# Two groups of 512 edges a step, and ScalarE copying the transposed sums out of two PSUM banks, in a graph layer on one core

## The chip, the cores and the metric

The kernel runs on one core of a Trainium2 chip. The metric is the device time of an execution in microseconds; the median of three runs before the change is 1433.29 us (1432.50 to 1433.74). The engines go by the profile's names: PE is TensorE (PEld its weight loads), DVE is VectorE, ACT is ScalarE, POOL is GpSimd, SP issues transfers.

## What is computed

One message-passing layer of a graph network with a residual and a layer norm: 6250 nodes of 128 features, 100000 edges sorted by destination. Cut to what matters:

```python
msg_in = concatenate([x[src], x[dst]])            # 100000 x 256
h = relu(msg_in @ Wm1 + bm1)                      # 256 wide
h = relu(h @ Wm2 + bm2)
messages = h @ Wm3 + bm3
agg = segment_sum(messages, dst) / clip(count, 1)
upd = relu(concatenate([x, agg]) @ Wn1 + bn1) @ Wn2 + bn2
out = layernorm(x + (x + upd))
```

## The kernel before

The kernel has three stages. The first makes two tables in memory from x: `atab`, x times the upper half of Wm1 (one row of 256 fp32 a node), and `btab`, x times the lower half, split into three bf16 terms. The second, the edge loop, goes over 196 groups of 512 edges (the last has 256 places). The third handles the nodes in blocks of up to 512.

In the edge loop a group is four subgroups of 128 edges. As the edges are sorted, the destinations of a subgroup lie in a window of 21 nodes (WB) that begins at a number read from `tilei`. For one group:

- `fetch` issues four gathers on POOL (L387), each 128 rows of `atab` by source into `ag`, and four transfers on SP (L393) of the windows' `btab` rows into `bw`. Both tiles have four buffers (pool `ld`), one a group.
- `destinations` issues, for two groups at a time, two transfers on ACT's queue (L328) that spread the destinations over partitions into `db`.
- `hot` makes on DVE two one-hot matrices by comparison: `oht` (L408), which picks `bw` rows for the edges, and `oh` (L411), which sums edges by destination.
- `first_layer` transposes the `ag` rows on PE into `ph` (L424, two halves of 64 rows side by side) and adds `bw` times `oht` there (L430). ACT adds the bias and clips (L435) into `h1`. `ph` has two banks, one for each half of a group (pool `p1`).
- `second_layer` multiplies `h1` by `w2` on PE (L444) into `ph2`, two banks, and DVE clips into `h2` (L446), of which there are four (NH2). A column of ones stands behind the 256 in `h2`, so that edges are counted with the sums.
- `sums` multiplies `oh` by `h2` on PE (L453) into the bank `pg` (pool `pa`, one), four strips of 32 rows, one a subgroup; ACT copies it to `part` (L456).
- `add_up` transposes `part` on PE (L464) into two banks `pt`, and DVE adds each window of 21 columns from `pt` to `acc` in SBUF (L469, four a group), at a place given by a register.

Each matmul in fp32 of L424, L444, L453 and L464 in the source stands as two instructions in the trace where it is a product (L444 has eight in the source and 16 in the trace), and as one where it is a transpose.

The order on PE is written out by hand (`tc.manual_schedule`): what the loop at L500 calls is what PE runs, in this order. The loop is a pipeline over groups with `ahead, lag = 2, 3`. Step i fetches group i, and with g = i - 2 then runs `hot` of g, `add_up` of g - 4, `first_layer` of g, `sums` of g - 3, `second_layer` of g - 1. So each step has one group in each function, every one from another group, and a product of ACT or DVE has about a step or more until PE reads it. On ACT, DVE, POOL and SP the tile framework places instructions by its own priorities; for ACT and DVE the order is that of the program until step 6 (`turns`). A buffer's next writer waits for its last reader, on whichever engine. [...]

Of the kernel before, what the change touches and what calls it, by code (L numbers as in the profile page):

```python
# [9 lines left out]
F32 = mybir.dt.float32  # L10
# [5 lines left out]
ENG = mybir.EngineType  # L16
PSUM = bass.MemoryType.PSUM
# [10 lines left out]
def kernel(  # L28
# [16 lines left out]
):  # L45

# [323 lines left out]
    with edge, tc.tile_pool(name="wk", bufs=2) as wk, tc.tile_pool(  # L370
        name="p1", bufs=2, space=PSUM
    ) as p1, tc.tile_pool(name="p2", bufs=2, space=PSUM) as p2, tc.tile_pool(
        name="pa", bufs=1, space=PSUM
    ) as pa, tc.tile_pool(name="pt", bufs=2, space=PSUM) as ptp:


        NH2 = 4
# [40 lines left out]
        def first_layer(ag, bw, oht, nt):  # L418
# [14 lines left out]
            for c in range(HC):  # L433
                for h in range(nh):
                    nc.scalar.activation(h1[:, c, h * 2 * P:(h + 1) * 2 * P], phs[h][:, c, :], AF.Relu,  # L435
                                         bias=b1[:, c:c + 1])
# [11 lines left out]
        def sums(oh, h2, nt):  # L448

            n = nt * WN  # L450
            pg = pa.tile([P, H + 1], F32, name="pg")
            for j in range(nt):
                nc.tensor.matmul(pg[j * WN:(j + 1) * WN, :], oh[:, j, :], h2[:, j, :],  # L453
                                 start=True, stop=True, skip_group_check=True)
            part = wk.tile([P, H + 1], F32, name="part")
            nc.scalar.copy(part[:n, :], pg[:n, :])  # L456
            return part

        def add_up(part, firsts, nt):
            pts = [ptp.tile([P, HC + 1, NQ], F32, name="pt") for _ in range(nt // 2)]  # L460
            for c in range(HC + 1):
                for h, pt in enumerate(pts):
                    rows = part[halves[h], c * P:(c + 1) * P] if c < HC else part[halves[h], H:].to_broadcast([NQ, P])
                    nc.tensor.matmul(pt[:, c, :], rows, ident[halves[h], halves[h]], is_transpose=True,  # L464
                                     start=True, stop=True, skip_group_check=True)
            for j, first in enumerate(firsts):
                window = acc[:, :, ds(first, WB)]
                k = j % 2 * WN
                nc.vector.tensor_add(window, window, pts[j // 2][:, :, k:k + WB])  # L469
# [28 lines left out]
        ahead, lag = 2, 3  # L498
        st = {}
        for i in range(NG + ahead + lag + 1):  # L500
            if i == 6:
                turns.close()
            if i == 16:
                late_loads()
                none = wk.tile([16, (NG * GE - E) // 16], I32, name="none", bufs=1)
                nc.vector.memset(none, NONE)
                nc.sync.dma_start(dpad[:E].rearrange("(p e) -> p e", p=16), dst.rearrange("(p e) -> p e", p=16))
                nc.sync.dma_start(dpad[E:].rearrange("(p e) -> p e", p=16), none)
            for step, after in enumerate((20, 24, 27)):
                if i >= after and (i - after) % 8 == 0 and (i - after) // 8 < len(pieces):  # L510
                    double((i - after) // 8, step)
            if i < NG:
                nt = GT if i < NGF else LT
                firsts = load_bases(tilei[0:1, i * GT:(i + 1) * GT], nt, ENG.SP)
                if i == NGF:
                    dbs = last_destinations()
                elif i % 2 == 0:
                    dbs = early.pop(0) if early else destinations(i, min(2, NGF - i), dst_row)
                st[i] = dict(nt=nt, got=fetch(srcT[:, i, :], nt, firsts), db=dbs.pop(0))
            g = i - ahead  # L520
            if 0 <= g < NG:
                s = st[g]
                ag, bw = s.pop("got")
                oht, s["oh"] = hot(s.pop("db"), pbase[:, g, :], dloc[:, g, :s["nt"]], s["nt"])
            k = g - lag - 1
            if 0 <= k < NG:
                s = st.pop(k)
                if "firsts" not in s:
                    s["firsts"] = load_bases(tilei[0:1, k * GT:(k + 1) * GT], s["nt"], ENG.DVE)
                add_up(s["part"], s["firsts"], s["nt"])  # L530
            if 0 <= g < NG:
                s = st[g]
                s["h1"] = first_layer(ag, bw, oht, s["nt"])
            k = g - lag
            if 0 <= k < NG:
                s = st[k]
                s["part"] = sums(s["oh"], s["h2"], s["nt"])
            m = g - 1
            if 0 <= m < NG:
                s = st[m]  # L540
                s["h2"] = h2s[m % NH2]
                second_layer(s["h1"], s["h2"], s["nt"])
            if m == NG - 1:
                for k in range(NG - lag, NG):
                    s = st[k]
                    s["firsts"] = load_bases(tilei[0:1, k * GT:(k + 1) * GT], s["nt"], ENG.DVE)
        assert not st
# [9 lines left out]
        with tc.For_i(0, groups, 1) as g:  # L557
# [3 lines left out]
            with tc.For_i(0, more, 1):  # L561
# [17 lines left out]
                add_up(sums(oh, h2s[0], GT), load_bases(ti, GT, ENG.DVE), GT)  # L579
# [132 lines left out]
```

## Time and profile before

| | us |
|---|---|
| median of the runs | 1433.29 |
| the profiled execution's own time | 1215.18 |
| its span, first to last instruction | 1213.4 |
| first L424 starts | 93.42 |
| last L444 block starts | 1128.24 |
| node stage's first matmul (L618) starts | 1136.67 |
| mean granted TensorE clock of the profiled execution | 0.991 |

The profiled execution is 218 us shorter than the median of the runs. Durations are read from the former. The page's group rows give, for a line and an engine, the instructions' count, their busy time and mean duration. The timeline gives the start, the duration from the first start to the last end, and how many instructions of one kind were merged; in brackets, idle time of the engine just before and what ended it. Matmuls overlap: the start of the next one says more than the duration[...]. "64\*128" ahead of a matmul's output is rows by columns of the array that it uses.

### The profile page before, as it was taken

To read this page: it belongs to the slowest core of one execution; us is meant where nothing else is said; L and a number is where in the kernel's file an instruction comes from. 1 tells how busy PE (TensorE), PEld (TensorE's weight loads), DVE (VectorE), ACT (ScalarE), POOL (GpSimd) and SP (SyncE) were. 2 spreads that over 40 slices of the span, in tenths; PEclk is the share of its full clock that TensorE was granted. 3 is DMA by queue.
4 is the path that set the end of the run, shared out by engine and by line. 5 is a ranking of instruction groups with operands and counts; after the bars stand their busy time and mean duration, and the time that the engine had idled before them with its cause. 6 is when DMAs were issued, how large, how long until landed. Compare 5 with 4: busy or idle time off the path is not lost. (4 is left out here: it accounts for less than half of the span.)

```text
span 1213.4 us, 32800 instructions
## 1 busy us (share of the span) xinstructions
PE 1181.3 (97%) x11196; PEld 898.6 (74%) x11197; DVE 675.1 (56%) x2085; ACT 446.8 (37%) x1158; POOL 804.7 (66%) x859
## 2 busy tenths in 40 slices
PE   7998999999999999999999999999999999999896
PEld 5746777777777777777777777777777777777565
DVE  5763555555555555555555555555555555555686
ACT  4553333333333333333333333333333333333256
POOL 8266776777777777777777777777777777673220
PEclk9998999999999999999999999999999999999898
DMA  9875666666555555555555555555555555552333
GB/s 270 295 255 148 188 186 186 180 187 179 154 153 153 151 152 153 144 152 151 153 153 151 151 152 149 145 155 153 153 151 152 153 152 146 148 152 69 96 110 105
DMA packets 178152, 193.66 MB, mean 160 GB/s; under 512 B 30844, under 2 KB 151374, under 8 KB 177968
## 3 DMA queue, kind: packets, MB, share of 16 engines
q0 software_dynamic: 37984, 103.35, 30.3%
q1 hardware_dynamic: 111436, 61.93, 17.9%
q10 hardware_dynamic: 28564, 26.27, 7.9%
q8 instruction: 90, 1.47, 0.5%
q14 instruction: 78, 0.64, 0.2%
HBM read 168.92 MB, written 22.88 MB: 158 GB/s over the span
## 5 line engine op out<-in xcount | busy, mean ns | idle before, releaser
L387 POOL DMA_INDIRECT ag<-atab,srcT x784 | 753.0, 960 | 288.9 <-issue 184.3
L444 PE MATMUL ph<-w,h 128*128 128x256 f32 x3128 | 729.7, 386 | 0.0
L444 PEld LDWEIGHTS ph<-w,h 128*128 128x128 f32 x3128 | 579.7, 190 | 151.8 <-DVE acc L469 69.9
L435 ACT ACTIVATE h<-ph,b 128x256 f32<-128x256 f32 x782 | 306.3, 474 | 673.8 <-PE ph L430 485.6
L446 DVE TENSOR_TENSOR h<-ph,nb 128x512 f32<-128x512 f32 x391 | 270.5, 692 | 418.0 <-PE ph L444 407.5
L469 DVE TENSOR_TENSOR acc<-acc,pt 128x63 f32 x782 | 171.8, 220 | 32.5 <-PE ph L430 2.7
L424 PE MATMUL ph<-ident,ag 64*128 64x64 f32 x3128 | 130.6, 223 | 2.9 <-ACT h L435 2.6
L453 PE MATMUL pg<-h,oh 128*32 128x257 f32 x1564 | 125.6, 392 | 0.0
L424 PEld LDWEIGHTS ph<-ident,ag 64*128 64x128 f32 x3128 | 113.7, 139 | 4.0 <-ACT h L435 2.9
L408 DVE TENSOR_SCALAR oht<-db,pbase 128x128 bf16<-128x128 int32 x392 | 105.4, 343 | 1.1 <-PE ph L430 0.7
L464 PEld LDWEIGHTS pt<-ident,part 64*128 64x128 f32 x1173 | 50.9, 136 | 66.6 <-issue 64.6
L456 ACT COPY part<-pg 128x257 f32<-128x257 f32 x196 | 76.5, 390 | 8.0 <-PE pg L453 8.0
L464 PE MATMUL pt<-ident,part 64*128 64x64 f32 x1173 | 77.8, 238 | 1.2 <-DVE acc L469 1.1
L430 PE MATMUL ph<-oht,bw 64*128 64x128 bf16 x1564 | 76.5, 217 | 0.7 <-DVE oht L408 0.7
L411 DVE TENSOR_TENSOR oh<-iota_n,dloc 128x128 f32<-128x128 f32 x196 | 55.1, 281 | 22.8 <-PE pg L453 22.4
L623 POOL TENSOR_TENSOR agg<-total,rc 128x512 f32<-128x512 f32 (+2 forms) x15 | 16.0, 1069 | 68.1 <-DMA rcol<-acc 31.6
L430 PEld LDWEIGHTS <-bw 64*128 64x128 bf16 x1564 | 53.7, 96 | 1.1 <-issue 0.9
L230 PE MATMUL pbt<-w,xT 128*128 128x256 f32 x196 | 48.6, 395 | 3.4 <-ACT bt L239 2.1
L453 PEld LDWEIGHTS pg<-h,oh 128*32 128x32 f32 x1564 | 30.8, 108 | 20.3
L230 PEld LDWEIGHTS pbt<-w,xT 128*128 128x128 f32 x196 | 36.8, 197 | 10.8 <-ACT bt L239 3.3
L250 POOL CAST bt<-rest 128x512 bf16<-128x512 f32 x18 | 11.8, 664 | 28.2 <-DVE rest L248 19.1
L645 PEld LDWEIGHTS pot<-wu,u 128*128 128x128 f32 (+1 forms) x196 | 24.0, 191 | 5.5 <-issue 4.8
(102 smaller groups left out, 412.4 us busy)
## 6 DMA issues: line engine op xcount, KB each, us to landing
bw<-btab SPq DMA_DIRECT2D x782, 32.0 KB
db<-in_dst_dram ACTq DMA_DIRECT2D x194, 128.0 KB
ag<-atab,srcT POOLq DMA_INDIRECT x784
btab<-bt SPq DMA_DIRECT2D x24, 384.0 KB
atab<-bt SPq DMA_DIRECT2D x24, 256.0 KB
xd<-in_x_dram SPq DMA_DIRECT2D x12, 256.0 KB
x2tab<-xd SPq DMA_DIRECT2D x12, 256.0 KB
x_sb<-in_x_dram SPq DMA_DIRECT2D x5, 512.0 KB
```

Of the source, the lines that this page charges most:

```text
L230: nc.tensor.matmul(pbt[:, a, :], xT[:, (t0 + a) * P:(t0 + a + 1) * P], w1[:, k, :], start=True, stop=True)
L387: nc.gpsimd.indirect_dma_start(out=ag[:, j, :], out_offset=None, in_=atab[:, :], in_offset=bass.IndirectOffsetOnAxis(ap=idx[:, j:j + 1], a ...
L408: nc.vector.tensor_scalar(oht[:n, k, :], db[:n, k * P:(k + 1) * P], pb_cols[:n, k:k + 1], None, op0=ALU.is_equal)
L424: nc.tensor.matmul(phs[h][:, c, u * NQ:(u + 1) * NQ], ag[halves[h], u, c * P:(c + 1) * P], ident[halves[h], halves[h]], is_transpose=True, ...
L430: nc.tensor.matmul(phs[h][:, c, k * P:(k + 1) * P], bw[halves[h], k, c * P:(c + 1) * P], oht[halves[h], k, :], start=False, stop=True, ski ...
L435: nc.scalar.activation(h1[:, c, h * 2 * P:(h + 1) * 2 * P], phs[h][:, c, :], AF.Relu, bias=b1[:, c:c + 1])
L444: nc.tensor.matmul(ph2[:, a, :], h1[:, c, (j0 + a) * P:(j0 + a + 1) * P], w2[:, c, :], start=(c == 0), stop=(c == HC - 1))
L446: nc.vector.tensor_tensor(h2[:, j0:j0 + 2, :H], ph2, nb2.to_broadcast([P, 2, H]), op=ALU.max)
L453: nc.tensor.matmul(pg[j * WN:(j + 1) * WN, :], oh[:, j, :], h2[:, j, :], start=True, stop=True, skip_group_check=True)
L456: nc.scalar.copy(part[:n, :], pg[:n, :])
L464: nc.tensor.matmul(pt[:, c, :], rows, ident[halves[h], halves[h]], is_transpose=True, start=True, stop=True, skip_group_check=True)
L469: nc.vector.tensor_add(window, window, pts[j // 2][:, :, k:k + WB])
```

## The change

Groups go in pairs: 98 steps (NS) instead of 196. A step fetches the next pair, then on PE runs `add_up` for both groups of the pair two steps back, `first_layer` for the one and the other group of this pair, `sums` for both groups of the pair before, and `second_layer` for both groups of this pair. `hot` of the next pair comes behind each `second_layer`. `h2` has two buffers, `ph` four banks (a half of a group each). `pg` and `pt` share one pool of two banks (tag "pa"): in a step first two `pt` tiles stand there, each of which holds one half of both groups, then two `pg` tiles, one a group. ACT copies each `pt` into a tile `col` in SBUF (384 elements a partition when full), and the DVE additions read `col`. ACT's relu loops are turned round, so that both parts of the first half come first. The steps of `double` and `late_loads` are set to the same groups as before. The window starts are loaded to registers for a pair at once, on SP and on DVE. The repeat loop at the end, which the inputs may need, calls `add_up` with one group.

```diff
@@ -368,13 +369,13 @@
         nc.sync.dma_start(bu2[:, 0, :], bn2.rearrange("(o h) -> o h", o=1).to_broadcast([P, D]))
 
     with edge, tc.tile_pool(name="wk", bufs=2) as wk, tc.tile_pool(
-        name="p1", bufs=2, space=PSUM
+        name="p1", bufs=4, space=PSUM
     ) as p1, tc.tile_pool(name="p2", bufs=2, space=PSUM) as p2, tc.tile_pool(
-        name="pa", bufs=1, space=PSUM
-    ) as pa, tc.tile_pool(name="pt", bufs=2, space=PSUM) as ptp:
-
-
-        NH2 = 4
+        name="pa", bufs=2, space=PSUM
+    ) as pa:
+
+
+        NH2 = 2
         h2s = [wk.tile([P, GT, H + 1], F32, name=f"h2_{i}", bufs=1) for i in range(NH2)]
         for t in h2s:
             nc.vector.memset(t[:, :, H:], 1.0)
@@ -430,8 +431,8 @@
                         nc.tensor.matmul(phs[h][:, c, k * P:(k + 1) * P], bw[halves[h], k, c * P:(c + 1) * P],
                                          oht[halves[h], k, :], start=False, stop=True, skip_group_check=True)
             h1 = wk.tile([P, HC, GE], F32, name="h1")
-            for c in range(HC):
-                for h in range(nh):
+            for h in range(nh):
+                for c in range(HC):
                     nc.scalar.activation(h1[:, c, h * 2 * P:(h + 1) * 2 * P], phs[h][:, c, :], AF.Relu,
                                          bias=b1[:, c:c + 1])
             return h1
@@ -448,7 +449,7 @@
         def sums(oh, h2, nt):
 
             n = nt * WN
-            pg = pa.tile([P, H + 1], F32, name="pg")
+            pg = pa.tile([P, H + 1], F32, name="pg", tag="pa")
             for j in range(nt):
                 nc.tensor.matmul(pg[j * WN:(j + 1) * WN, :], oh[:, j, :], h2[:, j, :],
                                  start=True, stop=True, skip_group_check=True)
@@ -456,17 +457,30 @@
             nc.scalar.copy(part[:n, :], pg[:n, :])
             return part
 
-        def add_up(part, firsts, nt):
-            pts = [ptp.tile([P, HC + 1, NQ], F32, name="pt") for _ in range(nt // 2)]
-            for c in range(HC + 1):
-                for h, pt in enumerate(pts):
-                    rows = part[halves[h], c * P:(c + 1) * P] if c < HC else part[halves[h], H:].to_broadcast([NQ, P])
-                    nc.tensor.matmul(pt[:, c, :], rows, ident[halves[h], halves[h]], is_transpose=True,
-                                     start=True, stop=True, skip_group_check=True)
-            for j, first in enumerate(firsts):
-                window = acc[:, :, ds(first, WB)]
-                k = j % 2 * WN
-                nc.vector.tensor_add(window, window, pts[j // 2][:, :, k:k + WB])
+        def add_up(parts, firsts, nts):
+
+            ng = len(parts)
+            pts = [pa.tile([P, ng, HC + 1, NQ], F32, name="pt", tag="pa") for _ in range(max(nts) // 2)]
+            for s, (part, nt) in enumerate(zip(parts, nts)):
+                for c in range(HC + 1):
+                    for h in range(nt // 2):
+                        rows = (part[halves[h], c * P:(c + 1) * P] if c < HC
+                                else part[halves[h], H:].to_broadcast([NQ, P]))
+                        nc.tensor.matmul(pts[h][:, s, c, :], rows, ident[halves[h], halves[h]], is_transpose=True,
+                                         start=True, stop=True, skip_group_check=True)
+            cols = []
+            for h, pt in enumerate(pts):
+                n = sum(nt // 2 > h for nt in nts)
+                col = wk.tile([P, 2, HC + 1, NQ], F32, name="col")
+                nc.scalar.copy(col[:, :n], pt[:, :n])
+                cols.append(col)
+            k = 0
+            for s, nt in enumerate(nts):
+                for j in range(nt):
+                    window = acc[:, :, ds(firsts[k], WB)]
+                    col = j % 2 * WN
+                    nc.vector.tensor_add(window, window, cols[j // 2][:, s, :, col:col + WB])
+                    k += 1
 
         def load_bases(ap, n, engine):
             _, firsts = nc.values_load_multi_w_load_instructions(
@@ -495,56 +509,65 @@
             else:
                 nc.sync.dma_start(rows(x2tab), twice.pop(k)[:r, :n])
 
-        ahead, lag = 2, 3
-        st = {}
-        for i in range(NG + ahead + lag + 1):
-            if i == 6:
+
+
+        NS = NG // 2
+        nts = [GT] * NGF + [LT]
+        gots, dbs, hots, h1s, ohs, parts = {}, {}, {}, {}, {}, {}
+
+        def pair(i):
+            return 2 * i, 2 * i + 1
+
+        def fetch_pair(i):
+            a, b = pair(i)
+            n = nts[a] + nts[b]
+            firsts = load_bases(tilei[0:1, a * GT:a * GT + n], n, ENG.SP)
+            for g in (a, b):
+                if g == NGF:
+                    dbs[g], = last_destinations()
+                elif g % 2 == 0:
+                    got = early.pop(0) if early else destinations(g, min(2, NGF - g), dst_row)
+                    dbs.update(zip((g, g + 1), got))
+                gots[g] = fetch(srcT[:, g, :], nts[g], firsts[:nts[g]])
+                firsts = firsts[nts[g]:]
+
+        def make_hot(g):
+            hots[g], ohs[g] = hot(dbs.pop(g), pbase[:, g, :], dloc[:, g, :nts[g]], nts[g])
+
+        fetch_pair(0)
+        for g in pair(0):
+            make_hot(g)
+        for i in range(NS + 2):
+            if i == 3:
                 turns.close()
-            if i == 16:
+            if i == 8:
                 late_loads()
                 none = wk.tile([16, (NG * GE - E) // 16], I32, name="none", bufs=1)
                 nc.vector.memset(none, NONE)
                 nc.sync.dma_start(dpad[:E].rearrange("(p e) -> p e", p=16), dst.rearrange("(p e) -> p e", p=16))
                 nc.sync.dma_start(dpad[E:].rearrange("(p e) -> p e", p=16), none)
-            for step, after in enumerate((20, 24, 27)):
-                if i >= after and (i - after) % 8 == 0 and (i - after) // 8 < len(pieces):
-                    double((i - after) // 8, step)
-            if i < NG:
-                nt = GT if i < NGF else LT
-                firsts = load_bases(tilei[0:1, i * GT:(i + 1) * GT], nt, ENG.SP)
-                if i == NGF:
-                    dbs = last_destinations()
-                elif i % 2 == 0:
-                    dbs = early.pop(0) if early else destinations(i, min(2, NGF - i), dst_row)
-                st[i] = dict(nt=nt, got=fetch(srcT[:, i, :], nt, firsts), db=dbs.pop(0))
-            g = i - ahead
-            if 0 <= g < NG:
-                s = st[g]
-                ag, bw = s.pop("got")
-                oht, s["oh"] = hot(s.pop("db"), pbase[:, g, :], dloc[:, g, :s["nt"]], s["nt"])
-            k = g - lag - 1
-            if 0 <= k < NG:
-                s = st.pop(k)
-                if "firsts" not in s:
-                    s["firsts"] = load_bases(tilei[0:1, k * GT:(k + 1) * GT], s["nt"], ENG.DVE)
-                add_up(s["part"], s["firsts"], s["nt"])
-            if 0 <= g < NG:
-                s = st[g]
-                s["h1"] = first_layer(ag, bw, oht, s["nt"])
-            k = g - lag
-            if 0 <= k < NG:
-                s = st[k]
-                s["part"] = sums(s["oh"], s["h2"], s["nt"])
-            m = g - 1
-            if 0 <= m < NG:
-                s = st[m]
-                s["h2"] = h2s[m % NH2]
-                second_layer(s["h1"], s["h2"], s["nt"])
-            if m == NG - 1:
-                for k in range(NG - lag, NG):
-                    s = st[k]
-                    s["firsts"] = load_bases(tilei[0:1, k * GT:(k + 1) * GT], s["nt"], ENG.DVE)
-        assert not st
+            for step, after in enumerate((10, 12, 13)):
+                if i >= after and (i - after) % 4 == 0 and (i - after) // 4 < len(pieces):
+                    double((i - after) // 4, step)
+            if i + 1 < NS:
+                fetch_pair(i + 1)
+            if i >= 2:
+                a, b = pair(i - 2)
+                n = nts[a] + nts[b]
+                firsts = load_bases(tilei[0:1, a * GT:a * GT + n], n, ENG.DVE)
+                add_up([parts.pop(a), parts.pop(b)], firsts, (nts[a], nts[b]))
+            if i < NS:
+                for g in pair(i):
+                    h1s[g] = first_layer(*gots.pop(g), hots.pop(g), nts[g])
+            if 1 <= i <= NS:
+                for g in pair(i - 1):
+                    parts[g] = sums(ohs.pop(g), h2s[g % NH2], nts[g])
+            if i < NS:
+                for g in pair(i):
+                    second_layer(h1s.pop(g), h2s[g % NH2], nts[g])
+                    if i + 1 < NS:
+                        make_hot(g + 2)
+        assert not (gots or dbs or hots or h1s or ohs or parts)
 
         order.close()
 
@@ -576,7 +599,7 @@
                 oht, oh = hot(db, pbc, dl, GT)
                 h1 = first_layer(ag, bw, oht, GT)
                 second_layer(h1, h2s[0], GT)
-                add_up(sums(oh, h2s[0], GT), load_bases(ti, GT, ENG.DVE), GT)
+                add_up([sums(oh, h2s[0], GT)], load_bases(ti, GT, ENG.DVE), (GT,))
 
 
     NB = 4 * P
```

## The prediction

> **What bounds the kernel now.** I read the busy table first.
>
> ```profile
> span 1213.4 us, 32800 instructions
> PE 1181.3 (97%) x11196; PEld 898.6 (74%) x11197; DVE 675.1 (56%) x2085; ACT 446.8 (37%) x1158; POOL 804.7 (66%) x859
> ```
>
> TensorE is busy for 97% of the span. Then the table by stretches, for 300 to 1000 us, the middle of the edge loop:
>
> ```profile
> 300.00:1000.00 700.00, 700.00 (x7180) 539.32 (x7180) 373.35 (x1197) 243.49 (x665) 508.31 (x532) 1.00 0.55 151
> ```
>
> It is busy without a break here, at the full clock (1.00). 532 gathers, four to a group of 512 edges, are 133 groups in 700 us: 5.26 us a group, and 196 x 5.26 = 1032 us of the 1213.4. What the period consists of is read from the starts in the timeline of TensorE:
>
> ```profile
> 705.75 0.40 PE L464 MATMUL pt<-ident,part 64*128 64x64 f32 x6
> 705.98 0.67 PE L424 MATMUL ph<-ident,ag 64*128 64x64 f32 x16
> 706.48 0.39 PE L430 MATMUL ph<-oht,bw 64*128 64x128 bf16 x8
> 706.80 0.64 PE L453 MATMUL pg<-h,oh 128*32 128x257 f32 x8
> 707.37 3.72 PE L444 MATMUL ph<-w,h 128*128 128x256 f32 x16
> 711.02 0.40 PE L464 MATMUL pt<-ident,part 64*128 64x64 f32 x6
> ```
>
> From start to start: L464 0.23 us, L424 0.50, L430 0.32, L453 0.57, L444 3.65, together 5.27. No step waits for another engine. But the array is used in three shapes (rows x columns: 64\*128, 128\*32, 128\*128), so each group changes shape three times. The price is in the gaps. An L444 matmul follows the one before by 0.216 us: two of them take 0.70 us in a narrow window and nine take 2.21, so seven more cost (2.21 - 0.70) / 7. The last of 16 starts at 707.37 + 3.72 - 0.38 = 710.71, and L464 at 711.02: 0.31 instead of 0.216, 0.09 lost. In the same way L430 to L453 loses 0.09 (last start 706.65, next 706.80, usual step 0.055) and L453 to L444 0.09 (last start 707.06, next 707.37, stream 0.216). After a change the first loads are bare too: the second L444 starts 0.32 after the first, 0.10 lost; L464 takes 0.23 where three pairs at 0.063 are 0.19, some 0.05 with its first gap; L453 loses 0.02. Together 0.44 us a group.
>
> The second thing to see is how close the gathers are:
>
> ```profile
> 606.79 0.95 POOL L387 DMA_INDIRECT ag<-atab,srcT  x1 [0.53 <-PE ph L430]
> 608.05 0.95 POOL L387 DMA_INDIRECT ag<-atab,srcT  x1 [0.30 <-issue]
> 609.31 0.96 POOL L387 DMA_INDIRECT ag<-atab,srcT  x1 [0.30 <-issue]
> 610.57 0.95 POOL L387 DMA_INDIRECT ag<-atab,srcT  x1 [0.30 <-issue]
> 612.06 0.96 POOL L387 DMA_INDIRECT ag<-atab,srcT  x1 [0.53 <-PE ph L424]
> ```
>
> A gather and the 0.30 us behind it are 1.26 us; four are 5.04. Only the 0.23 us more in every fourth gap is a wait for TensorE to free a buffer. The 66% of the table hides that POOL's floor is 96% of the period.
>
> [...] 0.09 us of empty array at each of the three changes, none from L464 to L424 to L430, which share 64 rows. [...] L411 is of that kind, and in the trace's records a gather that overlaps one takes 0.971 us against 0.957: there, but small.
>
> **The change part by part**, for a pair of groups.
>
> *Order on TensorE.* A pair now runs L464 for both, L424 and L430 for one group and then the other, L453 for both, L444 for both: three changes of shape a pair, not six. The matmuls are the same. The first group costs what it cost, 5.27. The second goes at stream price: L464 3 x 0.063 = 0.19, L424 0.50, L430 4 x 0.055 = 0.22 and 0.01 at its joint, L453 2 x 0.216 = 0.43, L444 16 x 0.216 = 3.46, sum 4.81. That is 10.08 us where it was 10.53: 0.45 saved, 98 x 0.45 = 44 us. L430 to the second group's L424 has no trace; it stays in 64 rows, and the way back costs nothing today, so I take 0. [...]
>
> *POOL.* The gathers and their four buffers stay. Eight need 8 x 1.26 = 10.08 us, exactly TensorE's new need. A buffer pair freed at one step is read two steps later, about 20 us on, while eight gathers and a landing take under 13, so POOL can run without stops. But it becomes as late as TensorE: any loss on it shows. The window additions (L469) read `col` in SBUF now instead of PSUM: eight a pair with two SBUF inputs. At L411's 0.014 us for each of the three or four gathers that they meet, 0.05 us: POOL's period is 10.13. Bounds: 0 and, if each of eight additions of 0.22 us fully blocked it, 1.76 us. The latter L411 excludes, 0.275 us long and costing 0.014; I keep 0.2 as the upper end. So the profiled step is 10.1 to 10.2; at 10.13 the gain is 40 us. I take 42 between the two floors.
>
> *ACT's copies of the transposed sums.* Two a pair, 384 elements[...]. ACT's work for a pair is then 8 relus at 0.39, 2 L456 at 0.39, 2 x 0.50, two issues of `db` at 0.63: 6.2 us of 10.1, hidden if it keeps the order. TensorE's side, from the start of L464: L464 ends at 0.42, its results at 0.6; copies end at 1.2 and 1.7. The sums (L453) want the two banks at 0.42 + 2 x 0.73 + 0.09 = 1.97, so they don't wait, by 0.3 us for the later bank. The relus of the first group then run 1.7 to 3.2, their first half done at 2.5; L444 wants that at 1.97 + 1.0 = 2.97. Before, a relu had a whole step; now it has 0.5 us of slack. The second group's relus end at 4.8, wanted at 6.4. The program's order on ACT is copies, eight relus, two L456, two `db` issues, so the issues end at 6.9, well before the next step at 10.1.
>
> *DVE.* L446 (four at 0.69), eight additions (0.26 apart, 2.1), oht and oh (0.54 + 0.28 twice) make 6.6 us of 10.1. The additions start at 1.3, and with the one-hots DVE is free at about 5.3; the first L446 is ready at 5.1, and its bank is wanted again at 6.4. It ends at 6.0. Queued behind the additions' wait for ACT are those L446; cover 0.4 us. The last L446 of a pair ends 0.9 into the next step; L453 wants it at 1.97, so two `h2` buffers are enough.
>
> *SP.* Eight bw transfers, 0.65 us from issue to issue, and one register load instead of two: 5.5 us of 10.1; nothing waits for it.
>
> *Ends.* Filling takes 22 us today for three second layers (93.4 to 115.5), with 2.6 us of stall for one `ph` pair; four banks remove that, but the first relu is exposed. At the end both kernels wait for the last sums, copies and additions. I put both at 0, +-4.
>
> Sum against the profiled execution: 1213.4 - 42 = 1171 us, a ratio of 0.966.
>
> **To the median.** The runs take 1433.3 us, 218 more than the profiled 1215.2. [...] If the 218 are a fixed addition, 1433 - 42 = 1391. If all scales, 0.966 x 1433.3 = 1384. I take 1384.
>
> **The rivals.**
> - *Half the gain*: POOL with 0.2 us of contention a pair, or DVE 0.25 us late for L444's bank. 98 x (0.45 - 0.22) = 22 us, 1433 - 1.1 x 22 = 1409. For it: both covers are thin. Against: L411's 0.014.
> - *No change*: the 218 us are slow gathers, which the profile doesn't show; then the timed period is 5.26 + 218/196 = 6.4 us, set by POOL, and the order on TensorE is worth nothing: 1432. Against: nothing in the profile makes a gather slower.
> - *Slower*: ACT is late. The two `db` issues, 1.26 us, wait for transfer slots and fall between the copies and the relus (in the pipeline's first steps the order has them so). The relu's first half comes at 3.8 where 2.97 is wanted: TensorE loses 0.8 a pair against 0.45 saved, 98 x 0.35 = 34, 1433 + 34 = 1467. It decides from 0.5 + 0.45, about 1 us of lateness on. Against: in the steady order the issues have 3 us to spare.
>
> **How the numbers follow.** The forecast has 0.71 (own range 1370 to 1400), half the gain 0.12, no change 0.08, slower 0.09. A measurement can tell about 0.2%, 3 us, from no change. Faster: 0.71 + 0.12 = 0.83; same: most of the third case, 0.07; slower 0.10 with its rest. The range goes from 1370 (a lower clock, a better fill) to 1412, just past half the gain; the last two cases stay outside.
>
> **What would show it.** Right: a period of 10.1 to 10.2 us a pair; one gap of 0.09 after L444 and after L453 for 32 and 16 matmuls; POOL's gaps nearly all 0.30 us; no idle of TensorE put down to ACT. Wrong: idle ahead of L453 or L444 that names `col` or `h`; gathers over 1.0 us; L424 waiting for a gather's landing. What would make the sum wrong is above all a timed run bound elsewhere than the profiled one.

## The result, and the profile after

The changed kernel takes 2112.66 us (median of four runs, 2102.8 to 2125.27) where the kernel before, beside it, takes 1432.89 (1432.36 to 1433.74): a ratio of 1.4748 [1.4667, 1.4829]. The forecast was 1384, the range 1370 to 1412. So the forecast had even the sign wrong.

The kernel before takes about 1216 us on some chips and about 1432 on others. The profile that I predicted from has the shorter time (1215.18), the runs the longer one, so they probably come from two chips; the record doesn't name these. I call the two kinds a 1216 chip and a 1433 chip.

Line numbers of the changed kernel are one higher up to `sums` (L424 is L425, L430 L431, L435 L436, L444 L445, L446 L447, L453 L454, L456 L457); the transposes of sums are L469 (L464 before), the new copies L475, the additions L482, the gathers L388. First its page:

```profile
span 2108.4 us, 32511 instructions
PE 1462.6 (69%) x11196; PEld 1036.7 (49%) x11197; DVE 669.3 (32%) x2083; ACT 532.0 (25%) x1354; POOL 806.1 (38%) x859
```

TensorE has the same 11,196 matmuls as before, but is busy for 69% of the span instead of 97%. POOL's work is what it was, 806 us. The same stretch of the edge loop as before (columns: stretch, length, busy time and instructions of PE, PEld, DVE, ACT, POOL, granted clock, DMA share, GB/s):

```profile
300.00:1000.00 700.00, 466.57 (x3776) 329.45 (x3777) 193.75 (x638) 157.34 (x416) 265.99 (x278) 0.84 0.28 81
```

278 gathers in 700 us are 2.52 us a gather: 20.1 us a pair of groups, where the sum said 10.1. The timeline of TensorE shows one pair:

```profile
1012.32 0.58 PE L469 MATMUL pt<-ident,part 64*128 64x64 f32 x12
1012.73 0.66 PE L425 MATMUL ph<-ident,ag 64*128 64x64 f32 x16
1013.23 0.39 PE L431 MATMUL ph<-oht,bw 64*128 64x128 bf16 x8
1013.46 0.66 PE L425 MATMUL ph<-ident,ag 64*128 64x64 f32 x16
1013.95 0.39 PE L431 MATMUL ph<-oht,bw 64*128 64x128 bf16 x8
1014.26 1.07 PE L454 MATMUL pg<-h,oh 128*32 128x257 f32 x16
1015.27 1.14 PE L445 MATMUL ph<-w,h 128*128 128x256 f32 x3
1016.66 0.59 PE L445 MATMUL ph<-w,h 128*128 128x256 f32 x2 [0.25 <-issue]
1018.11 0.69 PE L445 MATMUL ph<-w,h 128*128 128x256 f32 x2 [0.85 <-issue]
1019.52 1.24 PE L445 MATMUL ph<-w,h 128*128 128x256 f32 x5 [0.73 <-issue]
1020.96 1.13 PE L445 MATMUL ph<-w,h 128*128 128x256 f32 x4 [0.20 <-issue]
1026.72 6.13 PE L445 MATMUL ph<-w,h 128*128 128x256 f32 x16 [4.64 <-DVE h L447]
1032.79 0.58 PE L469 MATMUL pt<-ident,part 64*128 64x64 f32 x12
```

The steps up to 1015.27 stand as I had them: 2.95 us from the first transpose to the first L445 (the sum had 2.97). Then L445 comes in small lots with "issue" between, that is, waiting for nothing that the profile knows. The first group's 16 take 11.45 us to the start of the second group's instead of 3.55. The second group's 16 then take 6.07: ten of the steps between them are 0.427 us instead of 0.216, at half clock (the granted clock is 0.50 from 1024.84 to 1031.67). 7.9 and 2.5 us are the whole excess of 10.4. What the other engines do meanwhile is in the same table by stretches:

```profile
1012.30:1015.30 3.00, 3.00 (x78) 2.29 (x77) 2.25 (x9) 2.31 (x6) 1.32 (x2) 1.00 0.04 11
1015.30:1020.90 5.60, 3.63 (x16) 1.99 (x12) 0.45 (x3) 0.01 (x1) 4.38 (x5) 1.00 0.46 133
1020.90:1022.40 1.50, 1.13 (x4) 0.68 (x4) 0.49 (x2) 1.35 (x4) 1.02 (x2) 1.00 0.36 107
1022.40:1025.40 3.00, 0.00 (x0) 0.00 (x0) 0.00 (x0) 0.22 (x1) 0.96 (x1) 0.91 0.42 119
1025.40:1032.80 7.40, 6.08 (x18) 4.71 (x18) 2.38 (x5) 0.65 (x2) 0.00 (x0) 0.58 0.15 40
```

In the second row DVE and ACT nearly stop, and TensorE starts 16 matmuls where 26 would fit at 0.216 us; in the fourth row all three stop. The trace has SP take 6.31 us for three issues of `bw` from 1015.17 on, which are 0.65 us apart otherwise. Only POOL, the fifth of the busy columns, goes on at its own pace. Its timeline:

```profile
1013.67 0.95 POOL L388 DMA_INDIRECT ag<-atab,srcT  x1 [10.61 <-PE ph L431]
1014.93 0.98 POOL L388 DMA_INDIRECT ag<-atab,srcT  x1 [0.30 <-issue]
1016.22 0.96 POOL L388 DMA_INDIRECT ag<-atab,srcT  x1 [0.30 <-issue]
...
1022.53 0.96 POOL L388 DMA_INDIRECT ag<-atab,srcT  x1 [0.30 <-issue]
1034.14 0.95 POOL L388 DMA_INDIRECT ag<-atab,srcT  x1 [10.66 <-PE ph L431]
```

Eight gathers run 1.26 us apart, untouched. Then POOL waits 10.66 us for the next pair's L431 to free `ag`. So the two halves of the pair no longer overlap: for some 10 us the gathers go and the others mostly stand, for 10 us the others go and no gather does. I call it a pause when no engine but POOL starts anything for over 0.35 us, leaving out the steps of 0.425 us between matmuls at half clock, in which nothing stands. Over 90 inner pairs of the loop such pauses are 6.9 us a pair in this execution.

The kernel before pauses too on a 1433 chip, which the profile ahead of the prediction couldn't tell. TensorE's timeline of the kernel before there (b_third):

```profile
705.15 0.66 PE L424 MATMUL ph<-ident,ag 64*128 64x64 f32 x16
705.64 0.33 PE L430 MATMUL ph<-oht,bw 64*128 64x128 bf16 x5
706.66 0.27 PE L430 MATMUL ph<-oht,bw 64*128 64x128 bf16 x3 [0.69 <-issue]
706.87 0.64 PE L453 MATMUL pg<-h,oh 128*32 128x257 f32 x8
```

One such pause a group, in the middle of L430, with "issue" beside it. By the same count they are 1.0 us a group; the period is 6.40 us instead of 5.27, and 196 x 1.13 = 221 us are the gap that the prediction had to explain. TensorE's mean clock there is 0.99.

### The profile page after: what moved, and what is told of

It is laid out like the page before. It is cut to its first block, busy times and chain, and to the rows that moved or that the text cites. A ratio compares the mean times of both kernels' runs of the same rounds, so it can differ in the third digit from the quotient of the medians.

```text
span 2108.4 us, 32511 instructions
## 1 busy us (share of the span) xinstructions
PE 1462.6 (69%) x11196; PEld 1036.7 (49%) x11197; DVE 669.3 (32%) x2083; ACT 532.0 (25%) x1354; POOL 806.1 (38%) x859
## 5 line engine op out<-in xcount | busy, mean ns | idle before, releaser
L445 PE MATMUL ph<-w,h 128*128 128x256 f32 x3128 | 1032.6, 471 | 613.8 <-DVE h L447 367.6
L388 POOL DMA_INDIRECT ag<-atab,srcT x784 | 754.1, 962 | 1177.4 <-PE ph L431 908.5
L445 PEld LDWEIGHTS ph<-w,h 128*128 128x128 f32 x3128 | 712.5, 238 | 934.1 <-issue 534.9
L436 ACT ACTIVATE h<-ph,b 128x256 f32<-128x256 f32 x782 | 308.0, 484 | 520.5 <-remote 336.2
L447 DVE TENSOR_TENSOR h<-ph,nb 128x512 f32<-128x512 f32 x391 | 262.8, 688 | 539.5 <-PE ph L445 428.8
L475 ACT COPY col<-pt 128x384 f32<-128x384 f32 x196 | 84.2, 482 | 751.0 <-PE pt L469 729.0
L482 DVE TENSOR_TENSOR acc<-acc,col 128x63 f32 x782 | 174.7, 223 | 59.8 <-ACT col L475 37.4
L425 PE MATMUL ph<-ident,ag 64*128 64x64 f32 x3128 | 130.1, 223 | 0.4 <-ACT xT L345 0.4
L457 ACT COPY part<-pg 128x257 f32<-128x257 f32 x196 | 65.8, 384 | 218.2 <-remote 208.1
L425 PEld LDWEIGHTS ph<-ident,ag 64*128 64x128 f32 x3128 | 113.5, 139 | 1.1 <-issue 0.7
L454 PE MATMUL pg<-h,oh 128*32 128x257 f32 x1564 | 105.5, 386 | 0.6 <-ACT col L475 0.6
L431 PE MATMUL ph<-oht,bw 64*128 64x128 bf16 x1564 | 76.2, 216 | 0.1
L469 PEld LDWEIGHTS pt<-ident,part 64*128 64x128 f32 x1173 | 43.7, 138 | 33.5 <-issue 32.6
L469 PE MATMUL pt<-ident,part 64*128 64x64 f32 x1173 | 57.2, 230 | 0.3
L454 PEld LDWEIGHTS pg<-h,oh 128*32 128x32 f32 x1564 | 40.8, 109 | 28.4 <-ACT col L475 1.0
L431 PEld LDWEIGHTS <-bw 64*128 64x128 bf16 x1564 | 53.4, 96 | 0.2 <-issue 0.2
L231 PEld LDWEIGHTS pbt<-w,xT 128*128 128x128 f32 x196 | 37.0, 197 | 10.1 <-ACT bt L240 4.8
L641 PE MATMUL pmt<-acc,w 128*128 128x512 f32 (+2 forms) x60 | 24.9, 552 | 4.2 <-DVEq L580 4.2
```

The source lines that it names most:

```text
L231: nc.tensor.matmul(pbt[:, a, :], xT[:, (t0 + a) * P:(t0 + a + 1) * P], w1[:, k, :], start=True, stop=True)
L388: nc.gpsimd.indirect_dma_start(out=ag[:, j, :], out_offset=None, in_=atab[:, :], in_offset=bass.IndirectOffsetOnAxis(ap=idx[:, j:j + 1], a ...
L425: nc.tensor.matmul(phs[h][:, c, u * NQ:(u + 1) * NQ], ag[halves[h], u, c * P:(c + 1) * P], ident[halves[h], halves[h]], is_transpose=True, ...
L431: nc.tensor.matmul(phs[h][:, c, k * P:(k + 1) * P], bw[halves[h], k, c * P:(c + 1) * P], oht[halves[h], k, :], start=False, stop=True, ski ...
L445: nc.tensor.matmul(ph2[:, a, :], h1[:, c, (j0 + a) * P:(j0 + a + 1) * P], w2[:, c, :], start=(c == 0), stop=(c == HC - 1))
L447: nc.vector.tensor_tensor(h2[:, j0:j0 + 2, :H], ph2, nb2.to_broadcast([P, 2, H]), op=ALU.max)
```

## The experiments

Three explanations go by names in the texts of what was expected. "Burst": a long row of short TensorE instructions sets off the pauses. "Copy": ACT's copies and the shared banks cost the time. "Place": it depends on where the kernel runs.

Medians in us. The column "place" is what the kernel before takes on the same chip, beside the run.

| run | kernel | place | time | ratio |
|---|---|---|---|---|
| b_again, b_third | before | 1215.79, 1432.29 | 1215.99, 1433.08 | 1.0001 [0.9993, 1.001], 0.9996 [0.9978, 1.0014] |
| a_again, a_third | after | 1433.66, 1432.29 | 2117.07, 2123.4 | 1.4746 [1.47, 1.4791], 1.4832 [1.442, 1.5244] |
| a_fourth | after | 1215.47 | 1175.09 | 0.9664 [0.9636, 0.9692] |
| b_act | before, with ACT's copies | 1215.79 | 1213.9 | 0.9984 [0.9977, 0.9991] |
| a_split, a_split2 | after, TensorE group by group | 1215.79, 1432.29 | 1214.14, 1463.62 | 0.9985 [0.9978, 0.9992], 1.0223 [1.0179, 1.0267] |
| a_noact, a_noact2 | after, without ACT's copies | 1215.79, 1216.11 | 1312.68, 1312.91 | 1.0807 [1.077, 1.0845], 1.0797 [1.0761, 1.0832] |
| a_mid, a_mid2 | order between the two | 1215.47, 1216.11 | 1186.29, 1188.61 | 0.9757 [0.9724, 0.9789], 0.9775 [0.9696, 0.9853] |
| a_mid3 | the same | 1432.41 | 1906.51 | none given: 1872 to 1941 against 1429 to 1436 |
| b_dup | before, L424 twice | 1432.29 | 1530.69 | 1.0692 [1.0638, 1.0746] |
| b_quad | before, L424 four times | 1216.11 | 1504.77 | 1.2374 [1.2338, 1.241] |
| a_nogather, a_nogather2 | after, gathers for four groups only | 1215.47, 1216.11 | 1165.58, 1168.99 | 0.9586 [0.9558, 0.9614], 0.9613 [0.9585, 0.9641] |
| a_nogather3 | the same | 1430.74 | 1170.95 | 0.8182 [0.8156, 0.8208] |

**Part by part.** The change has two parts: ACT's copies with the shared banks, and TensorE's order. b_act puts the copies into the kernel before:

```diff
+            for pt in pts:
+                col = wk.tile([P, HC + 1, NQ], F32, name="col", bufs=4)
+                nc.scalar.copy(col, pt)
+                cols.append(col)
-                nc.vector.tensor_add(window, window, pts[j // 2][:, :, k:k + WB])
+                nc.vector.tensor_add(window, window, cols[j // 2][:, :, k:k + WB])
```

> The kernel before with one part of the change alone: ScalarE copies each bank of transposed sums to SBUF (192 elements, twice a group) and VectorE adds from the copy. Burst theory: the order on TensorE is that of before, so within 2% of 1433 us. Copy theory: clearly slower, 1600 us or more.

a_split keeps the change but for the order: transposed sums for a pair, then one group's first layer, sums and second layer with the lags of before, then the other's. For these lags it has three `h2` buffers instead of two, six of `oh` instead of four and three of `part` instead of two, which the lines below leave out.

```diff
-            if i < NS:
-                for g in pair(i):
+            for g in pair(i):
+                if g < NG:
                     h1s[g] = first_layer(*gots.pop(g), hots.pop(g), nts[g])
-            if 1 <= i <= NS:
-                for g in pair(i - 1):
...
+                if 0 <= g - 3 < NG:
+                    parts[g - 3] = sums(ohs.pop(g - 3), h2s[(g - 3) % NH2], nts[g - 3])
+                if 0 <= g - 1 < NG:
+                    second_layer(h1s.pop(g - 1), h2s[(g - 1) % NH2], nts[g - 1])
```

> The changed kernel with the copies, the shared banks and the paired additions kept, but TensorE's order split: first layer of one group, sums of the group three back, second layer of the group one back, then the same for the other group, so that a row of short instructions is 38 or 44 less its loads instead of 76. Burst theory: near the time of before, 1400 to 1500 us. Copy theory: stays near 2100 us.

> The changed kernel with TensorE's order split, as before, on the chip of the changed kernel. Burst theory: within 3% of the kernel before, whatever that is here. Place theory: the same where before takes 1433 us or where it takes 1216 us; it doesn't tell them apart alone, but beside the changed kernel it gives the price of the order on one chip.

a_noact is the changed kernel with `cols.append(pt)` in the place of the copy: DVE adds straight from the shared banks.

> The changed kernel without ScalarE's copies: VectorE adds the windows straight from the two shared banks, which are free only when the additions are done. Burst theory: the order on TensorE is the same, so it stays near 2100 us (2000 to 2250), with the 0.7 us pace on the sync queue. Copy theory: it falls back to about 1400 to 1500 us, some 1 us a pair being lost to the sums' wait for the additions.

b_act, a_split and a_noact fell on a 1216 chip, where nothing pauses, so the times that "burst" and "copy" had set for them didn't come. What they show is the price without pauses. The copies cost nothing there (1213.9, and 1214.14 for a_split). Without them the new order takes 97 us more than before, for the sums wait for their bank until DVE has done its additions, and some of them for ACT's copy to `part`. TensorE's timeline of a_noact, early in the loop:

```profile
310.49 0.64 PE L454 MATMUL pg<-h,oh 128*32 128x257 f32 x8 [0.96 <-DVE acc L480]
312.98 0.64 PE L454 MATMUL pg<-h,oh 128*32 128x257 f32 x8 [1.85 <-ACT part L457]
```

So the copies are what carries the order, and are hidden, as step "ACT's copies" had it. On a 1433 chip a_split2 costs 31 us more than before; the other 660 us of the changed kernel on that chip (a_third) belong to TensorE's order with the buffers that go with it. a_noact was never run on a 1433 chip (a_noact2 fell on a 1216 chip too).

**The same kernels again.** These show that the times repeat, and what the chip does.

> The kernel before, unchanged, for a trace taken beside the others. Burst theory (a long unbroken row of short TensorE instructions fills something that all engines issue through, after which every engine issues about one instruction in 0.7 us, and semaphore records go missing): this kernel's bursts are half as long, so its trace in these runs (1433 us) shows the same signs in a mild form, a few of the group steps longer than 5.3 us, and the 220 us above the first profiled execution are these. Copy theory (ScalarE's copies and the two shared banks cost the time): none of the signs here; the 220 us are a lower TensorE clock throughout[...] with even steps of 6.3 us.

> The kernel before, for a trace on the chip of the other three. If it takes 1433 us here, both theories that are left say that its trace shows stalls of all engines at once, at a pace of about 0.7 us on the sync queue, in a part of its groups; a lower TensorE clock is out, since its runs of 1433 us had a granted clock of 0.99.

> The changed kernel, unchanged, where the kernel before runs in 1216 us or in 1433 us, whichever these runs show. Burst theory: over 1.4 times the kernel before in either case, with the 0.7 us pace and missing records. Place theory (the runs that gave 1433 and 2112 us were made where recording or issue is slower for all engines; the changed kernel by itself has no such stall): where before takes 1216 us this kernel takes 1165 to 1185 us, steps of 10.1 to 10.2 us a pair, as predicted from the first profile.

> The changed kernel again, on the same chip as the next three. Burst theory: about 1.7 times the split order of the same call, wherever it runs. Place theory: near 2113 us if the kernel before takes 1433 us there, and 1165 to 1185 us if it takes 1216 us.

> The changed kernel unchanged, a fourth time. If the place decides (before takes 1216 in some places, 1433 in others), and this call lands where before takes 1216: 1165 to 1185 if my sum holds there (1171 was its result), and 2100 or more if the long row of short matmuls alone sets off the pauses. Where before takes 1433 it tells nothing new: about 2113.

The last one settles much: on a 1216 chip the changed kernel takes 1175.09. Its page, the stretch and TensorE's timeline:

```profile
span 1173.2 us, 32511 instructions
PE 1137.6 (97%) x11196; PEld 913.6 (78%) x11197; DVE 671.3 (57%) x2083; ACT 512.6 (44%) x1354; POOL 814.2 (69%) x859
```

```profile
300.00:1000.00 700.00, 699.69 (x7520) 573.93 (x7518) 388.06 (x1247) 300.16 (x832) 532.23 (x551) 1.00 0.58 157
```

```profile
704.38 0.58 PE L469 MATMUL pt<-ident,part 64*128 64x64 f32 x12
704.79 0.66 PE L425 MATMUL ph<-ident,ag 64*128 64x64 f32 x16
...
706.33 1.07 PE L454 MATMUL pg<-h,oh 128*32 128x257 f32 x16
707.33 7.17 PE L445 MATMUL ph<-w,h 128*128 128x256 f32 x32
714.44 0.58 PE L469 MATMUL pt<-ident,part 64*128 64x64 f32 x12
```

From L469 to L469 it is 10.06 us, with no idle time. The short steps take the same times as in the 2108 us execution; what differs is only what comes after 707.33.

**The length of the row.** b_dup and b_quad run each group's 16 L424 transposes two and four times (54 and 86 short matmuls in a row; the changed kernel has 76, the kernel before 38):

```diff
+            for again in range(2):
                 for c in range(HC):
                     for u in range(GT):
```

> The kernel before with the 16 transposes of each group (L424) run twice into the same place; the rest is the same, and the second pass writes what the first wrote. By the first profile the second pass streams for 0.50 us a group, 98 us in all. Burst theory: the row of short instructions is 54 instead of 38 and their records are more, so the time rises by much more than 98 us, by 300 us or more, with the signs of the changed kernel. Place theory where before takes 1216 us: 1314 us, no sign.

> Before with each group's 16 transposes of gathered rows done four times: 86 short matmuls in a row, more than the changed kernel's 76, but one group at a time. Twice cost 98 us, so four times cost 295 by streaming alone: 1728 where before takes 1433, 1511 where it takes 1216. If the length of the row sets off the pauses, then well above that where before takes 1433: 2100 or more.

b_dup's 98.4 us over 196 groups are 0.50 us each, the price of L424's stream, and its pauses are 1.0 us a group, as before: the longer row alone set off none. b_quad fell on a 1216 chip and shows no pause, so whether 86 in a row would bring them on a 1433 chip stays open. a_mid lets both first layers follow each other (60 in a row with the transposed sums), then one second layer, both sums, the other second layer:

```diff
+            for k in (b - 2,):
+                if 0 <= k < NG:
+                    second_layer(h1s.pop(k), h2s[1 + k // 2 % 2], nts[k])
+            for k in (a - 2, b - 4):
+                if 0 <= k < NG:
+                    parts[k] = sums(ohs.pop(k), h2s[0 if k % 2 == 0 else 1 + k // 2 % 2], nts[k])
+            if a < NG:
+                second_layer(h1s.pop(a), h2s[0], nts[a])
```

> The changed kernel with an order between the two: transposed sums and both first layers (60 short matmuls and their loads in a row), then one second layer, both sums (16 short ones), the other second layer; four changes of shape per pair instead of three (after) or six (before). Theory that the length of the row of short matmuls sets off the pauses: with 60 instead of 76 in a row, near the 54 of the doubled transposes that cost nothing extra, the kernel keeps a period near that of before: 1430 to 1500 where before takes 1433, about 1190 where before takes 1216 (two changes of shape saved per pair, 0.3 us each, 98 pairs: 29 us). Theory that it is the eight gathers and both groups' work being issued back to back, whatever the rows: the pauses stay, about 2000. Theory of my prediction (fewer changes of shape always pay): 1.5 to 2.5% faster than before in either place.

> The intermediate order again (60 short matmuls in a row, both first layers of a pair together, sums apart from them), for a place where before takes 1433. Theory that the length of the row of short matmuls sets off the pauses (54 cost nothing extra): between 1430 and 1600. Theory that two first layers released together, with their gathers, relus and one-hots, do it: about 2000. Where before takes 1216: about 1186 again.

> The intermediate order a third time, for a place where before takes 1433. Theory that the length of the row of short matmuls (60 here, 54 cost nothing extra, 76 brought the pauses) decides: 1430 to 1600, and at the lower end a version that loses nothing there and gains 29 us elsewhere. Theory that two groups released together decide: about 2000. Where before takes 1216: about 1187 again, and the question stays open.

On 1216 chips two changes of shape fewer a pair bring 28 to 29 us, as expected. On the 1433 chip the order costs 440 us in the one execution and 508 in the other, with pauses of 4.8 us a pair in the former, so this order isn't good in both places. That the length of the row decides, with 54 harmless and 60 nearly so, falls; that two groups' first layers follow each other fits, but their gathers' buffers come free together there too, and the two weren't told apart.

**The gathers.** a_nogather is the changed kernel, but the gathers of all groups after the fourth are left out: those groups read the first four groups' rows again.

```diff
+            if kept is not None and len(kept) == 4:
+                ag = kept[0]
+                kept.append(kept.pop(0))
...
-            for j in range(GT):
+            for j in range(GT) if fresh else ():
```

> The changed kernel, but GpSimd's gathers are issued for the first four groups only, and later groups take those groups' rows again; what it leaves out is the gathering of the source terms of all later groups. If the pauses come from the burst of TensorE's short matmuls alone, it still takes about 2000 or more. If they come from the gathers' issue or transfers lying on the same stretch, they go, and the kernel takes what TensorE's order needs: 1170 to 1250 in a place without pauses, up to 1450 where before has pauses of 1 us per group. If the gathers only add their issue time (10.1 us per pair), which is then hidden, nothing changes beside after.

> The changed kernel with gathers for the first four groups only (later groups take those rows again; it leaves out the later gathers), for a place where before takes 1433. If the pauses need the gathers' issue, their transfers or their landing events: 1165 to 1450. If TensorE's row alone does it: about 2000. Where before takes 1216: about 1166 again.

> The changed kernel with gathers for the first four groups only (it leaves out the later ones, whose rows are those of the first four), for a place where before takes 1433. The pauses stretch over the time in which eight gathers are issued and land; if these are needed for it (their transfers, descriptors or landing events), the kernel takes 1165 to 1450. If TensorE's order alone does it, about 2000. Where before takes 1216: 1167 again, and it stays open.

a_nogather3 decides. On a chip where before takes 1430.74, TensorE's new order without gathers takes 1170.95, near the 1165.58 and 1168.99 of 1216 chips, at a period of 10.06 us without a pause. The changed kernel with its gathers wasn't run on that chip. Its stretch:

```profile
300.00:1000.00 700.00, 700.00 (x7542) 574.55 (x7541) 387.67 (x1256) 301.90 (x837) 0.00 (x0) 1.00 0.19 54
```

But the one execution holds both cases, for 16 gathers are still made, the last at 89.26. Two stretches, 84 to 94 us and the next 10, first in a_nogather3, then in a_nogather:

```profile
84.00:94.00 10.00, 7.15 (x17) 2.78 (x16) 2.91 (x4) 2.64 (x4) 4.80 (x5) 1.00 0.36 100
94.00:104.00 10.00, 9.71 (x78) 7.00 (x77) 4.00 (x15) 4.71 (x11) 0.00 (x0) 0.83 0.19 51
```

```profile
84.00:94.00 10.00, 9.60 (x41) 4.90 (x40) 5.16 (x13) 4.23 (x7) 4.46 (x5) 1.00 0.44 126
94.00:104.00 10.00, 10.00 (x127) 8.68 (x126) 4.94 (x16) 3.71 (x10) 0.00 (x0) 1.00 0.27 75
```

While the gathers go, the 1433 chip runs 17 matmuls where the other runs 41, in a part of the kernel (L343) that has no rows of short matmuls at all. The first L425 (L435 there) comes at 98.94 us against 93.60; from then on the two run alike. The ends of the other loops fit: the period of the last pairs, for which nothing is left to fetch, falls from 20.6 us straight to 10.06 in the changed kernel, and that of the last groups of before on a 1433 chip from 6.39 to 5.27.

**What is shown, and what is open.** Shown: on a 1433 chip there are no pauses without gathers, and how much they cost depends on TensorE's order: 1.0 us a group before, 1.6 a pair in a_split2, 4.8 in a_mid3, 6.9 to 7.0 in the changed kernel, which pays for the half clock besides. In the changed kernel they hit every engine but POOL.

Not shown is what a gather and the other engines share there. It isn't simply the gather instruction on POOL: in b_third, from 300 to 1300 us, 196 of 199 pauses of over 0.45 us come after a group's fourth gather has been issued, and only two while a gather instruction runs. In the pair above POOL issues from 1013.67 to 1023.49, the gathers' packets move from 1015.3 to 1024.9 and the pauses last from 1016.0 to about 1025.4. Both point to what follows the issue, the transfers or the report of their landing, but no run takes these apart. One clue: in executions with pauses most records of semaphore updates are missing from the trace (12,692 in b_third against 33,922 in b_again; 14,758 in the changed kernel against 31,941 in a_fourth), nearly all of them those of DMA landings (9,079 against 29,222; 10,263 against 26,972), and in a_nogather3 hardly any are (23,022 against 23,404). Missing records and pauses go together here; which of them brings the other, or whether either does, no run shows. b_dup speaks against a mere count of records, since 32 more TensorE instructions a group, with their records, added no pause. But every execution on record was traced (each has its span and clock), so none shows whether a kernel pauses when nothing is recorded: that the tracing itself takes part stands as an untested rival. A fixed least time per gather falls: b_dup's stream would then have hidden in the 6.40 us. Spreading gathers apart was not tried, nor was the new order with gathers by another way.

## Why the prediction was wrong, point by point

- *Order on TensorE*: right, where gathers leave the engines alone. 10.06 us a pair (sum: 10.08), 0.48 less than twice 5.27 (0.45). The way from L431 to the second group's L425 costs nothing, as I took it; a_mid's fourth change of shape costs 10.26 - 10.06 = 0.20 us, where a third of the 0.44 for three changes is 0.15.
- *POOL*: right in size. Eight gathers are 10.11 us from start to start in a_fourth; its mean period is 10.12 with gathers and 10.06 without (a_nogather), so POOL is later than TensorE by 0.06 us a pair, 6 us in all. The forecast was 10.13. The reason given for it, 0.014 us more for a gather that overlaps an L411, isn't shown: over 300 to 1000 us of the profile before, gathers that overlap an L411 take 0.966 us on average and the others 0.956 (not 0.971 and 0.957), but a few long ones make this difference, and the medians are both 0.957; in a_fourth, gathers that overlap an addition take 0.967 us, like the others.
- *ACT's copies, DVE, SP*: right. The copies end 1.15 and 1.53 us after L469 starts (I had 1.2 and 1.7). The 0.50 us that I put down for a copy was my estimate; it is 0.48 (L475's mean in the 2108 us execution is 482 ns), halfway between the 0.37 and 0.59 of L239's copies of 256 and 512 elements in the profile before. L454 follows 1.95 us after L469 starts (1.97) and L445 at 2.95 (2.97); the issues of `db` end at 5.45, earlier than the 6.9 that I had. No idle of TensorE is put down to `col`.
- *The sum*: right. 1171 us against the span of 1173.2, a ratio of 0.966 against 0.9664.
- ***To the median*: this step failed.** I had 218 us that the profile didn't show, and took them to scale with the rest (1384), to be a fixed addition (1391) or, at the lower end of the range, a lower clock, all of which keep a gain of 42 us or more. They were none of these. The clock there is 0.99. The 218 us are pauses of 1.0 us a group that gathers bring, and the very thing that was changed, TensorE's order, makes them over three times as long, 6.9 us a pair instead of 2.0, and lets the clock fall to half besides (2.5 us in the pair shown). From the first L469 to the last the changed kernel takes 1895 us on the 1433 chip and 977 in a_fourth; these 918, and 18 ahead of the first, are the 935 us between the two spans (the rest ends 1 us earlier).
- *The rival "no change"* had the cause half right: gathers. Its period of 6.4 us follows from the gap, whatever the cause. But the gather isn't slow (964 ns in b_third, 960 in b_again) and POOL doesn't set the period: it waits 1.5 us a group for TensorE's L430. *The rival "slower"* (ACT late) didn't happen.
- The range was worked out from costs inside the profiled execution. That execution was 15% shorter than the runs, and what it doesn't hold can't be bounded from it. A case of unknown sign for that gap, with the gathers in it, would have had to stand in the range.

## What to carry to other kernels

Before you price a change from a profile, ask whether the profiled execution is the thing that is timed: if its own time and the median differ by more than they scatter, find what the difference is made of, or leave the sign open. When every engine but one stops at once with "issue" beside it, look at what the running one does, and take that work out in one experiment: here that told what the variations of the order had left open.

## What the hardware showed that was not expected

- The same program takes 1215 to 1216 us on three chips and 1431 to 1434 on three others (medians; single runs 1213.7 to 1218.3 and 1429.1 to 1437.9), at the same TensorE clock of 0.99. Only one chip, of the latter, was used at two times (1433.66 and 1432.29), so that it is the chip, and not something else about the place, is likely but not shown.
- On the latter, the gathers by indirect DMA from POOL bring pauses of TensorE, DVE, ACT and SP, 6.9 us a pair in the 2108 us execution, more than half of them 0.6 to 0.8 us long (201 of 357 from 300 to 1000 us), while POOL keeps its 1.26 us a gather.
- The pauses cost twice: after 4.6 us in which TensorE stood (1022.1 to 1026.7), the second group's matmuls start 0.427 us apart instead of 0.216 until the clock is back. The granted clock stays at 1.00 until 1024.84, 2.7 us after TensorE's last matmul ends, and is 0.50 from there to 1031.67. It is at 0.50 in 97 stretches of this execution, 75 of them of 6.8 us.
